# Expert rows in whole tiles of 256 and half tiles of 128, in place of whole tiles alone

## The chip, the core and the metric

The kernel runs on one NeuronCore of a Trainium2 chip. TensorE (PE) multiplies matrices and loads weights (PEld), VectorE (DVE), ScalarE (ACT) and GpSimd (POOL) work on elements, and SyncE (SP) issues most transfers. The metric is the device time of one execution, in microseconds (us). All data are fp32.

## The reference, cut to what matters

The reference is two layers of a model over 16 sequences of 569 rows (441 image tokens, 128 of text) with 256 columns: a tokenizer, windowed attention, a mixture of eight experts, a linear attention, and an LSTM over the 569 steps. The change is in the mixture of experts:

```python
xf = x.reshape(-1, Dd)                      # 9104 rows x 256
probs = jax.nn.softmax(xf @ gate_w + gate_b, axis=-1)
top2_vals, top2_idx = jax.lax.top_k(probs, 2)
cw = zeros.at[rows, top2_idx].add(top2_vals)
for w1, bb1, w2, bb2, we in zip(W1, b1, W2, b2, cw.T):   # 8 experts
    h = jax.nn.gelu(xf @ w1 + bb1)          # 256 -> 512
    y = h @ w2 + bb2                        # 512 -> 256
    acc = acc + we[:, None] * y
```

Only two of the eight weights `cw` of a row are not zero, so a kernel need run each row through two experts only.

## The kernel before

**Order of the work.** A first part (tokenizer, window attention, routing) holds about the first 950 us. It finds the two experts of every row and scatters each row, with its number, to the region of each expert in the DRAM tensor `XS` (L908, on POOL). Rows are padded to 72 chunks of 128, so there are 2 x 9216 = 18,432 rows for experts. Then the experts run, then the linear attention and the LSTM together to the end. The order of instructions on PE, DVE, ACT and POOL is written out when the program is built: a planner (`Order`) holds streams of steps with a cost each (`yield "PE", 0.43`) and picks the next step by the times at which engines come free. SP's order is the framework's. What runs is the order so built; engines wait on semaphores for what they need.

**Tiles.** How many rows an expert gets is known only at run time, but the number of tiles is fixed when the program is built. Each expert's rows are cut into tiles of `TILE` = 256. Eight experts can leave eight tiles partly filled, so `TILES` = 79 tiles are laid out, and all 79 always run.

**The plan of the tiles** (L1100 to L1155, on DVE) comes from `count`, the rows of each expert. `need` is the number of tiles of each expert and `end` its running sum. For every tile number, `past` marks the experts that end before it, so that its sum is the tile's `expert`, and `first` is its first row in `XS`. Both go to `where` as integers, which SP reads as register values (`planned`, L1158). The plan is worked out first for the four tiles that start, then for the other 75. `spare` gives row numbers to rows that hold nothing.

**A tile.** `tiles(slot)` is a stream; four of them (slots 0 to 3) take every fourth tile, and each has one PSUM bank. For a tile:

- SP loads `xs`, 256 rows of 258 columns (258 KB), and `w`, its expert's weights and biases (1154 KB), L1174 and L1168. Both have five buffers, so a tile's load waits for the tile five places earlier.
- PE turns the rows (`xtr`, four transposes, L1212), DVE copies them to `xt` (L1217). Four small DVE operations make the row numbers `to` (L1220 to L1233).
- The first layer, `hp` (L1241): the weights stand still and the 256 rows stream past, in two halves of four products each. After each half ACT applies gelu twice to give `hT` (L1248).
- The second layer, `y` (L1255): here 128 rows of `hT` stand still and the 256 columns of `w2` stream past, eight products.
- DVE adds the bias to give `ys` (L1261), and POOL scatters `ys` to the rows of `YT` in two indirect DMAs (L1184).

The linear attention's `front` later loads rows of `YT` (`yg`, L1353) and adds the two experts' results with their weights. `prepare` loads and prepares weights of later stages beside the experts.

Of the kernel before, what the change touches and what calls it, by code (L numbers as in the profile page):

```python
# [10 lines left out]
F32 = mybir.dt.float32  # L11
# [6 lines left out]
D = 256  # L18
# [3 lines left out]
E = 8  # L22
# [39 lines left out]

TILE = 256
REGION = [8 * 128 * len(g) + TILE for g in GROUPS]
TILES = [(2 * 8 * 128 * len(g) + E * (TILE - 1)) // TILE for g in GROUPS]
WPACK = 2 * HID + 4 + 4 * D + D

ROW = {n: i * D for i, n in enumerate(["bo", "b_out"])}
# [226 lines left out]
def kernel(ctx: ExitStack, tc: tile.TileContext, a: dict, out: bass.AP):  # L295
# [797 lines left out]
    def experts(g, mo, slots):  # L1093


        NT, most = TILES[g], E * REGION[g]
        bounded = "counts are bounded by the number of rows"

        behind = tiling.tile([128, E], mybir.dt.int32, name=f"behind{g}", tag="behind", bufs=1)
# [16 lines left out]
        warm = tiling.tile([128, 1], F32, name=f"warm{g}", tag="warm", bufs=1)  # L1116
        nc.scalar.activation(warm, count[:, :1], AF.Gelu)
        plan.table = "gelu"
        need = tiling.tile([128, E], F32, name=f"need{g}", tag="need", bufs=1)
        nc.vector.tensor_scalar(need, count, 1.0 / TILE, 0.5 - 0.5 / TILE, ALU.mult, ALU.add)  # L1120
        nc.vector.tensor_scalar(need, need, ROUND, None, ALU.add)
        nc.vector.tensor_scalar(need, need, ROUND, None, ALU.subtract)
        end = tiling.tile([128, E + 1], F32, name=f"end{g}", tag="end", bufs=1)
        nc.vector.memset(end[:, 0:1], 0.0)
        nc.vector.tensor_tensor_scan(end[:, 1:], ones[:, :E], need, 0.0, ALU.mult, ALU.add)
# [2 lines left out]
        first = tiling.tile([128, NT], F32, name=f"first{g}", tag="first", bufs=1)  # L1128
        where = tiling.tile([128, 2, NT], mybir.dt.int32, name=f"where{g}", tag="where", bufs=1)

        for lo, hi in ((0, slots), (slots, NT)):
            n, no = hi - lo, frow("tile_no", hi - lo, lo)
            past_, expert_, first_ = past[:, lo:hi], expert[:, lo:hi], first[:, lo:hi]
            nc.vector.tensor_tensor(
                past_, no.unsqueeze(2).to_broadcast([128, n, E]),
                end[:, 1:].unsqueeze(1).to_broadcast([128, n, E]), ALU.is_ge,
            )
            nc.vector.tensor_reduce(expert_, past_, AX.X, ALU.add)
            nc.vector.tensor_scalar(where[:, 1, lo:hi], expert_, float(E - 1), None, ALU.min)
            nc.vector.tensor_tensor(  # L1140
                past_, past_, need.unsqueeze(1).to_broadcast([128, n, E]), ALU.mult
            )
            nc.vector.tensor_reduce(first_, past_, AX.X, ALU.add)
            nc.vector.tensor_tensor(first_, no, first_, ALU.subtract)
            nc.vector.tensor_scalar(first_, first_, float(TILE), None, ALU.mult)
            nc.vector.scalar_tensor_tensor(
                first_, expert_, float(REGION[g]), first_, ALU.mult, ALU.add
            )
            nc.vector.tensor_scalar(where[:, 0, lo:hi], first_, float(most), None, ALU.min)

        spare = tiling.tile([128, 2, NT], F32, name=f"spare{g}", tag="spare", bufs=1)
        for i in range(2):
            nc.vector.tensor_scalar(
# [8 lines left out]

        loaded, bufs = [], slots + 1

        def weights(j, e=None):
            e = planned(1, j, j + 1, E - 1)[0] if e is None else e
            w = mo.tile([128, WPACK], F32, name=f"w{g}_{j}", tag="w", bufs=bufs)
            nc.sync.dma_start(w, a["wpack"][bass.ds(e, 1)].rearrange("e p n -> (e p) n"))  # L1168
            return w

        def load(j, w=None):
            at = planned(0, j, j + 1, most)[0]
            xs = mo.tile([128, 2, WIDE], F32, name=f"xs{g}_{j}", tag="xs", bufs=bufs)
            nc.sync.dma_start(xs, XS[g][bass.ds(at, TILE), :].rearrange("(i p) d -> p i d", p=128))  # L1174
            loaded.append((xs, weights(j) if w is None else w))

        ahead = [weights(j, e) for j, e in enumerate(planned(1, 0, 2, E - 1))]
# [1 line left out]
            load(j, ahead[j] if j < 2 else None)  # L1179

        def back_to_rows(j, ys, to):
            for i in range(2):
                yield "POOL", 1.27
                keep(nc.gpsimd.indirect_dma_start(  # L1184
                    out=YT, out_offset=bass.IndirectOffsetOnAxis(ap=to[:, i : i + 1], axis=0),
                    in_=ys[:, i, :], in_offset=None,
                ))
                nc.gpsimd.memset(between, 0.0)

        def tiles(slot):  # L1190
            for j in range(slot, NT, slots):
                while len(loaded) < min(j + 3, NT):
                    last = ("tile", g, len(loaded) - bufs)
                    if len(loaded) < bufs or last in plan.events:
                        load(len(loaded))
                    elif len(loaded) > j:
                        break
                    else:
                        yield "at", last
                yield "rank", j  # L1200
                xs, w = loaded[j]
                w1 = w[:, : 2 * HID].rearrange("p (k n) -> p k n", k=2)
                b1 = w[:, 2 * HID : 2 * HID + 4]
                w2 = w[:, 2 * HID + 4 : 2 * HID + 4 + 4 * D].rearrange("p (k n) -> p k n", k=4)
                b2 = w[:, 2 * HID + 4 + 4 * D :]
                if j < slots:
                    yield "pause", 5.0
                tr = bank(f"xtr{g}_{j}", slot).rearrange("p (k n) -> p k n", k=2)
                for k in range(2):
                    for i in range(2):  # L1210
                        yield "PE", TURN
                        nc.tensor.transpose(  # L1212
                            tr[:, k, 128 * i : 128 * i + 128], xs[:, i, 128 * k : 128 * k + 128], ident
                        )
                yield "DVE", 0.68
                xT = mo.tile([128, 2, TILE], F32, name=f"xt{g}_{j}", tag=f"xt{slot}", bufs=1)
                nc.vector.tensor_copy(xT, tr)  # L1217
                second = mo.tile([128, 2], F32, name=f"second{g}_{j}", tag=f"second{slot}", bufs=1)
                yield "DVE", 0.2
                nc.vector.tensor_scalar(  # L1220
                    second, xs[:, :, D + 1], expert[:, j : j + 1], float(KEPT),
                    ALU.not_equal, ALU.mult,
                )
                to = mo.tile([128, 2], mybir.dt.int32, name=f"to{g}_{j}", tag=f"rows{slot}", bufs=2)
                yield "DVE", 0.2
                nc.vector.tensor_tensor(second, second, xs[:, :, D], ALU.add)
                apart = mo.tile([128, 2], F32, name=f"apart{g}_{j}", tag=f"apart{slot}", bufs=1)
                yield "DVE", 0.2
                nc.vector.scalar_tensor_tensor(
                    apart, xs[:, :, D], 0.0, spare[:, :, j], ALU.is_equal, ALU.mult  # L1230
                )
                yield "DVE", 0.2
                nc.vector.tensor_tensor(to, second, apart, ALU.add)  # L1233
                hT = mo.tile([128, 4, TILE], F32, name=f"hT{g}_{j}", tag=f"hT{slot}", bufs=1)
                for half in range(2):
                    hp = bank(f"hp{g}_{j}_{half}", slot).rearrange("p (i n) -> p i n", i=2)
                    for i in range(2):
                        hc = 2 * half + i
                        for k in range(2):
                            yield "PE", 256 * COLUMN  # L1240
                            nc.tensor.matmul(  # L1241
                                hp[:, i, :], w1[:, k, hc * 128 : (hc + 1) * 128], xT[:, k, :],
                                start=(k == 0), stop=(k == 1),
                            )
                    for i in range(2):
                        hc = 2 * half + i
                        yield "ACT", 0.47, "gelu"
                        nc.scalar.activation(  # L1248
                            hT[:, hc, :], hp[:, i, :], AF.Gelu, bias=b1[:, hc : hc + 1]
                        )  # L1250
                y = bank(f"y{g}_{j}", slot).rearrange("p (i n) -> p i n", i=2)
                for i in range(2):
                    for hc in range(4):
                        yield "PE", 256 * COLUMN
                        nc.tensor.matmul(  # L1255
                            y[:, i, :], hT[:, hc, 128 * i : 128 * i + 128], w2[:, hc, :],
                            start=(hc == 0), stop=(hc == 3),
                        )
                yield "DVE", 0.69
                ys = mo.tile([128, 2, D], F32, name=f"ys{g}_{j}", tag=f"ys{slot}", bufs=2)  # L1260
                nc.vector.tensor_tensor(ys, y, b2.unsqueeze(1).to_broadcast([128, 2, D]), ALU.add)  # L1261
                plan.mark(("tile", g, j))
                plan.fork(back_to_rows(j, ys, to))

        return [tiles(slot) for slot in range(slots)]
# [810 lines left out]
```

## Time and profile before

| | |
|---|---|
| median of 3 runs | 3378.91 us (3378.6 to 3380.3) |
| profiled execution | 3360.87 us |
| its span, first to last instruction | 3359.0 us |
| mean TensorE clock granted | 0.978 |
| busy share of the span: PE, DVE, ACT, POOL | 91%, 60%, 44%, 23% |
| experts, first transpose to last `ys` | 972.8 to 1577 us |

A busy share is over the whole span; the stages differ. A row of the profile's groups gives the line, the engine, the operation with output and inputs, the count, the busy time and the mean of one instruction, and then the idle time just before, with what ended it. PE's records overlap, so that the time of a row of products is read from the step between their starts. An fp32 product of the code stands as two records, a transpose as one.

### The profile page before, as it was taken

Reading aid. Unit: us, or ns where it says so; the run is one execution under the profiler, and the core shown is the slowest. Engines: PE = TensorE matmul, PEld = TensorE weight load, DVE = VectorE, ACT = ScalarE, POOL = GpSimd, SP = SyncE. Lnnn points to the kernel's source line nnn. Section 1 sums busy time; section 2 is a strip of 40 time slices with the busy share of each in tenths; the row PEclk is TensorE's granted clock in tenths of the full one; section 3 lists DMA queues with packets and bytes.
Section 4 is the critical chain, followed back from the end, with each engine's and each line's share of the span. In section 5 each row is a group of like instructions: output and inputs, shape, how many; then the busy total and the mean of one; then the engine's idle time right before and its main releaser. Section 6 shows DMA issues by size and latency. Waiting matters only on the chain.

```text
span 3359.0 us, 134328 instructions
## 1 busy us (share of the span) xinstructions
PE 3055.1 (91%) x57536; PEld 2231.5 (66%) x57536; DVE 2027.2 (60%) x6787; ACT 1471.9 (44%) x5030; POOL 786.6 (23%) x1524
## 2 busy tenths in 40 slices
PE   5999999999859999997899999999999999999884
PEld 3666666666548888886566676766666666666652
DVE  4677777766732222222566777777777777766555
ACT  3545545454412222221444555555555555554442
POOL 1243554445533322232311001010101010100000
PEclk9999999999979999998999999999999999999997
DMA  5111221111176666664333333333333333333333
GB/s 180 53 46 57 89 79 54 55 38 41 42 251 234 220 231 225 225 229 141 100 100 88 90 82 86 84 94 78 97 77 92 84 93 79 76 91 80 90 103 113
DMA packets 276070, 366.81 MB, mean 109 GB/s; under 512 B 144480, under 2 KB 220176, under 8 KB 263312
## 3 DMA queue, kind: packets, MB, share of 16 engines
q1 hardware_dynamic: 249360, 300.91, 30.5%
q0 software_dynamic: 14496, 39.75, 3.1%
q10 hardware_dynamic: 11616, 17.56, 1.8%
q8 instruction: 451, 7.39, 0.9%
q14 instruction: 147, 1.20, 0.1%
HBM read 239.33 MB, written 118.75 MB: 107 GB/s over the span
## 4 chain that ended last, share of the span: by engine, by line
PE 37%; DVE 7%; ACT 5%; issue 2%; SPq 1%; DMA 1%; POOL 0%; ACTq 0%; DVEq 0%; POOLq 0%
PE gates L1741 13%; PE xm_False L1085 5%; PE out_gate L1750 2%; PE ek L1085 2%; PE po_False L1085 2%; PE z L1085 2%; PE v L1085 2%; PE eq L1085 2%; PE ds_False L1085 2%; ACT act L1762 1%; PE r_False L1085 1%; ACT th L1798 1%; DVE ab L1777 1%; DVE cT L1790 1%; DVE act L1783 1%
## 5 line engine op out<-in xcount | busy, mean ns | idle before, releaser
L1741 PE MATMUL gates<-W_hh,X 128*16 128x96 f32 (+1 forms) x18176 | 487.9, 248 | 63.9 <-DVE X L1805 61.6
L1741 PEld LDWEIGHTS gates<-W_hh,X 128*16 128x16 f32 (+1 forms) x18176 | 373.6, 103 | 258.5 <-DVE X L1805 245.0
L1248 ACT ACTIVATE hT<-hp,w 128x256 f32<-128x256 f32 x316 | 132.6, 472 | 481.5 <-PE hp L1241 314.5
L1762 ACT ACTIVATE act<-gates 128x96 f32<-128x96 f32 x568 | 142.1, 250 | 444.1 <-PE gates L1741 437.0
L1255 PE MATMUL y<-w,hT 128*128 128x256 f32 x1264 | 289.7, 382 | 5.2 <-ACT hT L1248 1.5
L1085 PE MATMUL xm_False<-W_ih,dxT_False 128*32 128x256 f32 x4352 | 292.3, 380 | 2.3 <-DVE dxT_False L1271 1.9
L1241 PE MATMUL hp<-xt,w 128*128 128x256 f32 x1264 | 287.6, 381 | 1.0 <-ACT hT L1248 1.0
L1777 DVE SCALAR_TENSOR_TENSOR ab<-act 128x64 f32<-128x64 f32 x568 | 127.9, 225 | 258.2 <-ACT act L1762 250.8
L1255 PEld LDWEIGHTS y<-w,hT 128*128 128x128 f32 x1264 | 236.8, 190 | 45.2 <-ACT hT L1248 14.4
L1684 PEld LDWEIGHTS <-nil 128*32 128x32 bf16 x4552 | 190.3, 94 | 111.0 <-issue 53.0
L1241 PEld LDWEIGHTS hp<-xt,w 128*128 128x128 f32 x1264 | 239.9, 191 | 35.7 <-ACT hT L1248 1.5
L1184 POOL DMA_INDIRECT YT<-ys,to x158 | 153.4, 971 | 440.4 <-DVE ys L1261 408.9
L1261 DVE TENSOR_TENSOR ys<-y,w 128x512 f32<-128x512 f32 x79 | 54.6, 691 | 316.3 <-PE y L1255 241.1
L1750 PE MATMUL out_gate<-W_hh,X 128*32 128x64 f32 x9088 | 233.8, 219 | 0.7 <-issue 0.7
L1690 ACT COPY gates<-xc 128x96 f32<-128x96 f32 x569 | 138.6, 244 | 182.0 <-DMA xc<-XCD 75.4
L1750 PEld LDWEIGHTS out_gate<-W_hh,X 128*32 128x32 f32 x9088 | 187.9, 110 | 2.9 <-issue 1.1
L1805 DVE SCALAR_TENSOR_TENSOR X<-toT,th 128x32 f32<-128x32 f32 x569 | 109.9, 193 | 120.5 <-ACT th L1798 116.9
L1798 ACT ACTIVATE th<-cT 128x32 f32<-128x32 f32 x569 | 130.5, 229 | 92.9 <-DVE cT L1790 43.1
L1301 POOL TENSOR_SCALAR d_False_rstd<-d_False_mv 128x2 f32<-128x2 f32 (+1 forms) x36 | 9.0, 250 | 671.8 <-DVE d_False_mv L1293 547.4
L908 POOL DMA_INDIRECT XS<-XN,at x144 | 149.1, 1035 | 45.6 <-issue 24.6
L693 PE MATMUL wqk<-wxT,wqkv 128*128 128x128 f32 x1152 | 150.6, 278 | 8.9 <-ACT wxT L687 8.6
L693 PEld LDWEIGHTS wqk<-wxT,wqkv 128*128 128x128 f32 x1152 | 139.4, 192 | 24.9 <-ACT wxT L687 13.5
(356 smaller groups left out, 6497.9 us busy)
## 6 DMA issues: line engine op xcount, KB each, us to landing
w<-in_wpack SPq DMA_DIRECT2D x79, 1154.0 KB
taps<-in_taps SPq DMA_DIRECT2D x16, 1764.0 KB
xc<-XCD SPq DMA_DIRECT2D x71, 384.0 KB
XCD<-xp_False SPq DMA_DIRECT2D x256, 96.0 KB
xs<-XS SPq DMA_DIRECT2D x79, 258.0 KB
yg<-YT SPq DMA_DIRECT2D x72, 256.0 KB
HD<-h SPq DMA_DIRECT2D x72, 128.0 KB
fh<-HD SPq DMA_DIRECT2D x72, 128.0 KB
```

The costliest lines, as they stand in the source:

```text
L693: nc.tensor.matmul(qk[:, j, m, :], wqkv[:, k, D * j + 128 * m : D * j + 128 * m + 128], xT[:, k, :], start=(k == 0), stop=(k == 1),)
L908: fill(0, nc.gpsimd.indirect_dma_start(out=XS[0], out_offset=bass.IndirectOffsetOnAxis(ap=at[:, i, c - lo : c - lo + 1], axis=0), in_=XN[p ...
L1085: nc.tensor.matmul(out[own], lhsT[:, own], rhs, start=start, stop=stop)
L1184: keep(nc.gpsimd.indirect_dma_start(out=YT, out_offset=bass.IndirectOffsetOnAxis(ap=to[:, i : i + 1], axis=0), in_=ys[:, i, :], in_offset= ...
L1241: nc.tensor.matmul(hp[:, i, :], w1[:, k, hc * 128 : (hc + 1) * 128], xT[:, k, :], start=(k == 0), stop=(k == 1),)
L1255: nc.tensor.matmul(y[:, i, :], hT[:, hc, 128 * i : 128 * i + 128], w2[:, hc, :], start=(hc == 0), stop=(hc == 3),)
L1684: nc.tensor.matmul(g[32 * q : 32 * q + 32, :n], nil[:, :32], nil[:, :n], start=True, stop=last)
L1741: nc.tensor.matmul(GC[32 * q : 32 * q + NB * (1 + half), :96], before[:, kk, NB * (1 - half) :], Whh[:, kk, own : own + 96], start=False, ...
L1750: nc.tensor.matmul(GO[32 * q : 32 * q + 32, :64], before[:, kk, :], Whh[:, kk, own : own + 64], start=False, stop=(kk == 1),)
L1762: nc.scalar.activation(act[:, :96], GC[:, :96], AF.Tanh, scale=0.5), begun.pop((k, t))
L1777: nc.vector.scalar_tensor_tensor(ab, act[:, :64].rearrange("p (g x) -> p g x", g=2), 1.0, act[:, 64:].rearrange("p (g x) -> p g x", g=2), ...
L1798: nc.scalar.activation(th.rearrange("p k x -> p (k x)"), cT, AF.Tanh, scale=0.5)
```

## The change

Experts' rows are cut into half tiles of 128 rows. Of each expert as many whole tiles of 256 as fit (`need`, now half of `halves` rounded down) come first. At least 68 whole tiles exist whatever the counts, so 68 whole tiles and 15 half tiles are laid out (`WHOLE` = 68, `TILES` = 83) and all 83 run. The half tiles take what the 68 whole ones leave: `left` is the number of halves of each expert that no whole tile holds. Their plan is a third block on DVE, after the blocks of 4 and of 64 whole tiles.

The 15 half tiles (numbers 68 to 82) are spread by `order`: the first comes after tile 7, then one after every four whole tiles, the last before tile 64. The loads, the slots and the planner's ranks go by the place in this order, no more by the number of the tile. A half tile loads 128 rows and its expert's full weights, and does two transposes, `hp` with 128 columns, four `y` products and one scatter. The planner's costs are scaled to match.

```diff
-TILES = [(2 * 8 * 128 * len(g) + E * (TILE - 1)) // TILE for g in GROUPS]
+WHOLE = [(2 * 8 * 128 * len(g) - E * TILE // 2 + TILE - 1) // TILE for g in GROUPS]
+TILES = [
+    w + (2 * 8 * 128 * len(g) + E * (TILE // 2 - 1)) // (TILE // 2) - 2 * w for w, g in zip(WHOLE, GROUPS)
+]
...
+        half = TILE // 2
+        halves = tiling.tile([128, E], F32, name=f"halves{g}", tag="halves", bufs=1)
         need = tiling.tile([128, E], F32, name=f"need{g}", tag="need", bufs=1)
-        nc.vector.tensor_scalar(need, count, 1.0 / TILE, 0.5 - 0.5 / TILE, ALU.mult, ALU.add)
-        nc.vector.tensor_scalar(need, need, ROUND, None, ALU.add)
-        nc.vector.tensor_scalar(need, need, ROUND, None, ALU.subtract)
+        for to, x, by, off in (
+            (halves, count, 1.0 / half, 0.5 - 0.5 / half), (need, halves, 0.5, -0.25)
+        ):
+            nc.vector.tensor_scalar(to, x, by, off, ALU.mult, ALU.add)
+            nc.vector.tensor_scalar(to, to, ROUND, None, ALU.add)
+            nc.vector.tensor_scalar(to, to, ROUND, None, ALU.subtract)
...
-        for lo, hi in ((0, slots), (slots, NT)):
+        for lo, hi in ((0, slots), (slots, whole)):
...
+        n, no = NT - whole, frow("tile_no", NT - whole)
+        past_, expert_, first_ = past[:, whole:], expert[:, whole:], first[:, whole:]
...
+        nc.vector.tensor_scalar(begin, end, float(whole), 2.0, ALU.min, ALU.mult)
+        nc.vector.memset(used[:, E:], 0.0)
+        nc.vector.tensor_tensor(used[:, :E], begin[:, 1:], begin[:, :E], ALU.subtract)
+        nc.vector.tensor_tensor(left, halves, used[:, :E], ALU.subtract)
+        nc.vector.tensor_tensor_scan(end[:, 1:], ones[:, :E], left, 0.0, ALU.mult, ALU.add)
...
+        nc.vector.tensor_scalar(where[:, 0, whole:], first_, float(most), None, ALU.min)
...
+        def rows_in(j):
+            return 2 if j < whole else 1
+
+        each = (whole - 2 * slots) / (NT - whole)
+        order = sorted(
+            range(NT), key=lambda j: j if j < whole else 2 * slots - 0.5 + (j - whole) * each
+        )
...
-        def load(j, w=None):
+        def load(n, w=None):
+            j = order[n]
...
-            nc.sync.dma_start(xs, XS[g][bass.ds(at, TILE), :].rearrange("(i p) d -> p i d", p=128))
+            n = rows_in(j)
+            nc.sync.dma_start(
+                xs[:, :n, :], XS[g][bass.ds(at, 128 * n), :].rearrange("(i p) d -> p i d", p=128)
+            )
...
-            for i in range(2):
+            for i in range(rows_in(j)):
                 yield "POOL", 1.27
...
-            for j in range(slot, NT, slots):
-                while len(loaded) < min(j + 3, NT):
+            for at, j in list(enumerate(order))[slot::slots]:
+                while len(loaded) < min(at + 3, NT):
...
                 for k in range(2):
-                    for i in range(2):
+                    for i in range(n):
                         yield "PE", TURN
...
-                            yield "PE", 256 * COLUMN
+                            yield "PE", 128 * n * COLUMN
                             nc.tensor.matmul(
-                                hp[:, i, :], w1[:, k, hc * 128 : (hc + 1) * 128], xT[:, k, :],
+                                hp[:, i, : 128 * n], w1[:, k, hc * 128 : (hc + 1) * 128], xT[:, k, :],
                                 start=(k == 0), stop=(k == 1),
...
-                        yield "ACT", 0.47, "gelu"
+                        yield "ACT", 0.25 + 0.11 * n, "gelu"
...
-                for i in range(2):
+                for i in range(n):
                     for hc in range(4):
                         yield "PE", 256 * COLUMN
...
-                yield "DVE", 0.69
+                yield "DVE", 0.14 + 0.275 * n
...
-                plan.mark(("tile", g, j))
+                plan.mark(("tile", g, at))
```

More of the change, by code (lines that the diff above doesn't have):

```diff
@@ L1093, in experts @@
     def experts(g, mo, slots):
-        NT, most = TILES[g], E * REGION[g]
+        NT, whole, most = TILES[g], WHOLE[g], E * REGION[g]
         bounded = "counts are bounded by the number of rows"
@@ L1149, in experts @@
             nc.vector.tensor_scalar(where[:, 0, lo:hi], first_, float(most), None, ALU.min)
+        n, no = NT - whole, frow("tile_no", NT - whole)
+        past_, expert_, first_ = past[:, whole:], expert[:, whole:], first[:, whole:]
+        used = tiling.tile([128, E + 1], F32, name=f"used{g}", tag="used", bufs=1)
+        begin = tiling.tile([128, E + 1], F32, name=f"begin{g}", tag="begin", bufs=1)
+        left = tiling.tile([128, E], F32, name=f"left{g}", tag="left", bufs=1)
+        nc.vector.tensor_scalar(begin, end, float(whole), 2.0, ALU.min, ALU.mult)
[3 more added lines that the diff above has]
+        nc.vector.tensor_tensor_scan(end[:, 1:], ones[:, :E], left, 0.0, ALU.mult, ALU.add)
+        nc.vector.tensor_tensor(begin[:, 1:], used[:, 1:], used[:, :E], ALU.subtract)
+        nc.vector.tensor_tensor(begin[:, 1:], begin[:, 1:], left, ALU.subtract)
+        nc.vector.tensor_tensor(
+            past_, no.unsqueeze(2).to_broadcast([128, n, E]),
+            end[:, 1:].unsqueeze(1).to_broadcast([128, n, E]), ALU.is_ge,
+        )
+        nc.vector.tensor_reduce(expert_, past_, AX.X, ALU.add)
+        nc.vector.tensor_scalar(where[:, 1, whole:], expert_, float(E - 1), None, ALU.min)
+        nc.vector.tensor_tensor(
+            past_, past_, begin[:, 1:].unsqueeze(1).to_broadcast([128, n, E]), ALU.mult
+        )
+        nc.vector.tensor_reduce(first_, past_, AX.X, ALU.add)
+        nc.vector.tensor_tensor(first_, no, first_, ALU.add)
+        nc.vector.tensor_scalar(first_, first_, used[:, :1], float(half), ALU.add, ALU.mult)
+        nc.vector.scalar_tensor_tensor(
+            first_, expert_, float(REGION[g]), first_, ALU.mult, ALU.add
+        )
+        nc.vector.tensor_scalar(where[:, 0, whole:], first_, float(most), None, ALU.min)
         spare = tiling.tile([128, 2, NT], F32, name=f"spare{g}", tag="spare", bufs=1)
@@ L1163, in experts @@
         loaded, bufs = [], slots + 1
+        def rows_in(j):
[3 more added lines that the diff above has]
+            range(NT), key=lambda j: j if j < whole else 2 * slots - 0.5 + (j - whole) * each
+        )
         def weights(j, e=None):
@@ L1169, in weights @@
             return w
-        def load(j, w=None):
+        def load(n, w=None):
+            j = order[n]
             at = planned(0, j, j + 1, most)[0]
             xs = mo.tile([128, 2, WIDE], F32, name=f"xs{g}_{j}", tag="xs", bufs=bufs)
-            nc.sync.dma_start(xs, XS[g][bass.ds(at, TILE), :].rearrange("(i p) d -> p i d", p=128))
+            n = rows_in(j)
+            nc.sync.dma_start(
+                xs[:, :n, :], XS[g][bass.ds(at, 128 * n), :].rearrange("(i p) d -> p i d", p=128)
+            )
             loaded.append((xs, weights(j) if w is None else w))
@@ L1195, in tiles @@
                         load(len(loaded))
-                    elif len(loaded) > j:
+                    elif len(loaded) > at:
                         break
@@ L1199, in tiles @@
                         yield "at", last
-                yield "rank", j
-                xs, w = loaded[j]
+                yield "rank", at
+                xs, w = loaded[at]
+                n = rows_in(j)
                 w1 = w[:, : 2 * HID].rearrange("p (k n) -> p k n", k=2)
@@ L1214, in tiles @@
                         )
-                yield "DVE", 0.68
+                yield "DVE", 0.14 + 0.27 * n
                 xT = mo.tile([128, 2, TILE], F32, name=f"xt{g}_{j}", tag=f"xt{slot}", bufs=1)
-                nc.vector.tensor_copy(xT, tr)
+                xT = xT[:, :, : 128 * n]
+                nc.vector.tensor_copy(xT, tr[:, :, : 128 * n])
                 second = mo.tile([128, 2], F32, name=f"second{g}_{j}", tag=f"second{slot}", bufs=1)
@@ L1220, in tiles @@
                 nc.vector.tensor_scalar(
-                    second, xs[:, :, D + 1], expert[:, j : j + 1], float(KEPT),
+                    second[:, :n], xs[:, :n, D + 1], expert[:, j : j + 1], float(KEPT),
                     ALU.not_equal, ALU.mult,
@@ L1225, in tiles @@
                 yield "DVE", 0.2
-                nc.vector.tensor_tensor(second, second, xs[:, :, D], ALU.add)
+                nc.vector.tensor_tensor(second[:, :n], second[:, :n], xs[:, :n, D], ALU.add)
                 apart = mo.tile([128, 2], F32, name=f"apart{g}_{j}", tag=f"apart{slot}", bufs=1)
@@ L1229, in tiles @@
                 nc.vector.scalar_tensor_tensor(
-                    apart, xs[:, :, D], 0.0, spare[:, :, j], ALU.is_equal, ALU.mult
+                    apart[:, :n], xs[:, :n, D], 0.0, spare[:, :n, j], ALU.is_equal, ALU.mult
                 )
                 yield "DVE", 0.2
-                nc.vector.tensor_tensor(to, second, apart, ALU.add)
+                nc.vector.tensor_tensor(to[:, :n], second[:, :n], apart[:, :n], ALU.add)
                 hT = mo.tile([128, 4, TILE], F32, name=f"hT{g}_{j}", tag=f"hT{slot}", bufs=1)
@@ L1246, in tiles @@
                         hc = 2 * half + i
-                        yield "ACT", 0.47, "gelu"
+                        yield "ACT", 0.25 + 0.11 * n, "gelu"
                         nc.scalar.activation(
-                            hT[:, hc, :], hp[:, i, :], AF.Gelu, bias=b1[:, hc : hc + 1]
+                            hT[:, hc, : 128 * n], hp[:, i, : 128 * n], AF.Gelu, bias=b1[:, hc : hc + 1]
                         )
                 y = bank(f"y{g}_{j}", slot).rearrange("p (i n) -> p i n", i=2)
-                for i in range(2):
+                for i in range(n):
                     for hc in range(4):
@@ L1258, in tiles @@
                         )
-                yield "DVE", 0.69
+                yield "DVE", 0.14 + 0.275 * n
                 ys = mo.tile([128, 2, D], F32, name=f"ys{g}_{j}", tag=f"ys{slot}", bufs=2)
-                nc.vector.tensor_tensor(ys, y, b2.unsqueeze(1).to_broadcast([128, 2, D]), ALU.add)
-                plan.mark(("tile", g, j))
+                nc.vector.tensor_tensor(
+                    ys[:, :n], y[:, :n], b2.unsqueeze(1).to_broadcast([128, n, D]), ALU.add
+                )
+                plan.mark(("tile", g, at))
                 plan.fork(back_to_rows(j, ys, to))
```

## The prediction

> **What bounds the kernel now.** I read the page's groups first, to find the lines that the change touches, then the busy time by stretches, then the instructions of one loop turn in order of time, and last who waits for whom.
>
> The groups (line, engine, operation, tiles, count | busy, mean ns | idle before):
>
> ```profile
> L1255 PE MATMUL y<-w,hT 128*128 128x256 f32 x1264 | 289.7, 382 | 5.2 <-ACT hT L1248 1.5
> L1241 PE MATMUL hp<-xt,w 128*128 128x256 f32 x1264 | 287.6, 381 | 1.0 <-ACT hT L1248 1.0
> L693 PE MATMUL wqk<-wxT,wqkv 128*128 128x128 f32 x1152 | 150.6, 278 | 8.9 <-ACT wxT L687 8.6
> L693 PEld LDWEIGHTS wqk<-wxT,wqkv 128*128 128x128 f32 x1152 | 139.4, 192 | 24.9 <-ACT wxT L687 13.5
> ```
>
> The two expert products have 1264 records each, 16 per tile of 79: every fp32 product that the code writes is two records. L693 belongs to another stage; it shows the same product at 128 columns instead of 256, each with its own weights, which is what a half tile's first layer will be. Busy time of PE, PEld, DVE, ACT, POOL, clock, DMA share and GB/s, by stretches:
>
> ```profile
> 972.00:1000.00 28.00, 25.65 (x113) 22.14 (x114) 6.43 (x24) 5.75 (x14) 4.29 (x8) 0.84 0.80 283
> 1000.00:1540.00 540.00, 535.07 (x2576) 464.44 (x2575) 131.37 (x453) 119.26 (x284) 166.47 (x304) 1.00 0.67 228
> 1540.00:1577.00 37.00, 33.77 (x158) 28.37 (x156) 6.75 (x20) 7.56 (x18) 9.99 (x20) 1.00 0.20 67
> ```
>
> The experts run from 972.8 to 1577, 18% of the span. In their middle PE is busy 535 of 540 us, the transfers 0.67. One loop turn, PE alone (start, duration):
>
> ```profile
> 1194.85 0.81 PE L1241 MATMUL hp<-xt,w 128*128 128x256 f32 x3
> 1195.50 1.04 PE L1212 MATMUL xtr<-ident,xs 128*128 128x128 f32 x8
> 1196.64 3.72 PE L1255 MATMUL y<-w,hT 128*128 128x256 f32 x16
> 1200.20 3.19 PE L1241 MATMUL hp<-xt,w 128*128 128x256 f32 x14
> 1203.22 3.62 PE L1255 MATMUL y<-w,hT 128*128 128x256 f32 x16
> 1206.68 4.05 PE L1241 MATMUL hp<-xt,w 128*128 128x256 f32 x18
> ```
>
> The transposes at 1180.44 and at 1195.50 are one turn apart: 15.06 us for two tiles, **7.53 us a tile**. Records overlap; what counts is the step between starts. 18 products in 4.05 with the last one 0.38 long: 3.67 / 17 = 0.2155 us a record. 8 transposes: (1.04 - 0.27) / 7 = 0.109. A tile is then 32 x 0.2155 + 4 x 0.109 = 7.33 us of PE, and 0.20 is left over. 0.27 per turn of that stands before the y at 1196.64, where PE waits for ACT's gelu; the rest is 0.065 a tile. So in this stage PE's rows are the time, and the next stage starts when the last YT rows have landed.
>
> Who waited, in SP's own waits from 1000 to 1560 (total, times, longest), and, ahead of the stage, from 940 to 975:
>
> ```profile
> SPq L1168 <- DVE ys L1261: 402.1, 71, 6.9
> ```
>
> ```profile
> SPq L1158 <- DVE where L1149: 11.8, 1, 11.8
> SPq L1168 <- DMA XS<-XN,at: 10.1, 5, 3.3
> ```
>
> SP waits for a buffer to come free before nearly every weight load: loads are ahead of PE, not behind it.
>
> **What the Trainium skill says.** "TensorE: Matmul & The Clock Gate", Back-to-back issue gap, gives a warm step of N / 2.4 + 2.5 ns, nearly proportional to the columns N. The trace agrees in form at two passes per record: 256 columns would be 216 ns (measured 215.5), 128 would be 109. Its part What happens when you issue a matmul, first step, says that the next weights load while the present matmul runs; here the 192 ns loads of L693 run under steps shorter than they are (below). "DMA: Bandwidth & Descriptors", Anatomy of one DMA, puts about 2 us on a transfer beside its bytes, measured for GpSimd's path; the loads here are SP's, and for them I use what this trace shows, 5.1 us in all for an xs (below).
>
> **The change, part by part.** 68 whole and 15 half tiles are 19,328 rows, 79 whole ones 20,224: 11 whole tiles go, 15 half tiles come.
>
> *A half tile on PE.* First layer: 8 products, 16 records of 128 columns. Their step is measured on L693, 16 records in one run:
>
> ```profile
> 442.48 2.00 PE L693 MATMUL wqk<-wxT,wqkv 128*128 128x128 f32 x16
> ```
>
> (2.00 - 0.275) / 15 = 0.115; an 18-record run (2.17) and a 1.95 one give 0.1115, which I take. 16 x 0.1115 = 1.78. Second layer: the weights and rows change places, so it stays at 256 columns and halves in number: 8 x 0.2155 = 1.72. Transposes 2 x 0.109 = 0.22. Sum **3.73 us**, against 7.33.
>
> *A turn.* In the changed kernel's instruction order a turn is four whole tiles and one half: 4 x 7.33 + 3.73 = 33.05. Waits for gelu: in the turn shown above the y at 1196.64 came 1.57 us after PE had issued the last hp it needs (1191.62, the start of the 18-run before it, + 16 x 0.2155 = 1195.07), with 1.30 of other work between (two records and 8 transposes), because a gelu of the next tile sits between its own two on ACT. In the new turn one y has this pattern and only two records and 6 transposes between, 1.08: it waits 0.49. The other four have 1.29 or more between and need two gelus running, 1.57 - 0.42 = 1.15: no wait. Leftover 5 x 0.065 = 0.3. Turn: 33.05 + 0.5 + 0.3 = 33.85. 15 turns 507.8, the other 8 whole tiles 8 x 7.53 = 60.2, together 568.0. Before: 79 x 7.53 = 594.9. **Gain 26.9 us.**
>
> *The plan of the tiles on DVE.* Three more 128x8 operations ahead of the first `where` (0.16 to 0.17 each): 0.5 us later. Then a block of 64 instead of 75 columns (0.1 less on each of four) and 16 small operations for the half tiles, about 3.2 us. Hidden: the first weight load waits until 963.4 for the XS rows to land, while the first `where` was there at 952.5, so some 10 us cover the 0.5; DVE's next work is xt at 973.9, the plan ends about 960. Without that cover the 0.5 would count. Taken as 0, bounds 0 to +0.5. POOL's scatter to XS waits for the cast of `at`, which stands one place earlier in DVE's order: 0.
>
> *SP and the transfers.* Four more tiles are 8 more DMAs with as many register loads; SP stands idle 402 us, so 0. One Wq load moves ahead of the first w, into SP's wait from 940.7: 0. Bytes per tile 1.18 MB of weights whole or half, 0.264 or 0.132 of rows in and about as much out. Weights +4.7 MB, rows -1.8: about 2% more bytes in 568 instead of 595 us, the share goes from 0.67 to 0.72. The shortest lead is that of the third whole tile of a group of three: its xs is issued after the ys of the tile six places earlier. From that y's end PE does hp 1.72, 0.89, 0.43, y 3.45, hp 0.89, 1.29, y 1.72, hp 1.72 and 8 transposes 0.87, 13.0 us; less ys (0.9 with its hop) and SP's load of w before it (0.8) leaves 11.3 us. An xs needed 5.1 us in the flood at the start (xs of tile 3 issued 972.00, PE's transposes of it at 977.09, four weight loads about it, share 0.80). So 6 us in hand: 0, and for the worst see the rivals.
>
> *ACT, DVE and POOL inside the stage.* Half-size gelu, copies and adds, 151 scatters for 158: these engines are busy 22, 24 and 31%, all less than before. 0.
>
> *After the experts.* The last four tiles are whole as before, so the tail (last y, ys, two scatters, the yg loads) is the same. PE's, ACT's and POOL's order in the LSTM stage is unchanged; on DVE six operations of one front, and one yg load on SP, come a few places later, once. They stand beside a chain of gates with waits of 100 us and more on those streams: 0, bounds -1 and +2.
>
> Sum: -26.9. The profiled run took 3360.87 (span 3359.0 + 1.9), 18 us less than the median 3378.91 of the three runs (3378.6 to 3380.3). I take the difference over to the median: **3352.0**.
>
> **The rivals.**
> 1. *Gelu waits vanish altogether* in the new order (leftovers too): 15 x 33.05 + 8 x 7.33 = 554.4, which is 40 less; half of that extra is as far as I believe: 3345. For it: longer runs of transposes. Against it: order on ACT. Chance 0.12.
> 2. *A 128-column step limited by its weight load*, 0.190 instead of 0.1115, if the w tile's loads don't overlap as L693's do: 15 x 16 x 0.0785 = 18.8 back, gain 8: 3371. Against it: L693 has the same 192 ns loads with other weights each time. Chance 0.07, with half steps between.
> 3. *The loads become the bound, and the kernel slower.* A half tile's weights come for half the PE time: its bytes, 1.45 MB at 339 GB/s (228 at a share of 0.67), are 4.3 us of transfer for 3.73 of PE. If the third xs of each group landed later than its lead, PE would stop once a turn. It eats the gain at 26.9 / 15 = 1.8 us a turn, that is a landing 13.1 us after issue, and is slower by 0.2% from 13.6 us; at 14.5 it gives 15 x 3.2 = 48, so 3400. For it: five weight loads in 33.85 us instead of 4.5. Against it: over a turn 24.5 us of transfer in 33.85, and the 5.1 us at the start. Chance 0.05.
> 4. *The half tiles do less than said*: if the planner had put them together rather than spread, waits for weights would follow; the built order shows one per turn, so this falls under 3.
>
> Likeliest, as computed, with losses of a few us from transfers or the later stage: 0.76, 3346 to 3360.
>
> **How the numbers follow.** A run of this kernel can tell about 0.2%, 6.8 us. Low end 3343: rival 1 and a little. High end 3365: N = 128 at 0.125 (+3.2), half a us of xs wait a turn (+8), +2 from the LSTM stage. Faster by over 0.2% (below 3372.1): all but rival 3 and the tail of 2: 0.93; same 0.03; slower 0.04.
>
> **What would show it.** Page after: 1328 hp records (68 x 16 at 256 columns, 15 x 16 at 128) and 1208 y records (68 x 16 + 15 x 8), the 128-column ones stepping 0.11; five tiles in 33.9 us; the stage from 973 to about 1550; PE's wait for xs only at the start; SP still waiting for ys. Wrong if PE waits for xs or w in each turn, if the first xtr comes later than 973.5, or if the LSTM stage's length changes by over 3 us.

## The result, and the profile after

| | before | after |
|---|---|---|
| median of 5 runs | 3378.91 us | 3349.33 us |
| lowest to highest | 3378.2 to 3382.1 | 3346.3 to 3353.5 |
| ratio, 95% interval | | 0.9913 [0.9899, 0.9927] |
| profiled execution (span) | 3360.87 (3359.0) | 3353.51 (3351.6) |

The change takes 29.6 us off; 26.9 were forecast. The two profiled executions differ by only 7 us: that of before was 18 us under its median and that of after the slowest of its five. So their spans are not subtracted here; they are read stage by stage.

The page's groups of after, the two expert products (count | busy, mean ns | idle before):

```profile
L1306 PE MATMUL y<-w,hT 128*128 128x256 f32 x1208 | 276.3, 381 | 6.9 <-ACT hT L1299 6.4
L1292 PE MATMUL hp<-xt,w 128*128 128x256 f32 (+1 forms) x1328 | 275.2, 360 | 0.0
```

1208 and 1328 records are the numbers forecast. The second form of `hp` is the 128-column one. The page now names gelu for 6.4 us of waits at L1306, where it named it for 1.5 at L1255. That is not more waiting in all: the 0.27 that a turn of before loses at one `y` leaves gaps too short for the page to name. By the prediction's readings 39 such turns lose about 10.5 us (an estimate), and 15 turns of after at 0.49 lose about 7.4.

The middle of the stage by the busy-time view (PE, PEld, DVE, ACT, POOL, clock, DMA share, GB/s):

```profile
1000.00:1540.00 540.00, 535.05 (x2717) 471.87 (x2716) 139.11 (x497) 126.75 (x318) 167.47 (x305) 1.00 0.70 243
```

PE is as full as before (535.05 against 535.07 us of 540), and the transfers' share went from 0.67 to 0.70.

PE alone in order of time, one turn of four whole tiles and one half (start, duration, and in brackets the idle time before):

```profile
1225.42 2.35 PE L1292 MATMUL hp<-xt,w 128*128 128x128 f32 x14
...
1245.76 2.32 PE L1292 MATMUL hp<-xt,w 128*128 128x256 f32 x10
1247.92 0.82 PE L1262 MATMUL xtr<-ident,xs 128*128 128x128 f32 x6
1249.06 3.72 PE L1306 MATMUL y<-w,hT 128*128 128x256 f32 x16 [0.32 <-ACT hT L1299]
1252.61 3.21 PE L1292 MATMUL hp<-xt,w 128*128 128x256 f32 x18
1255.67 3.62 PE L1306 MATMUL y<-w,hT 128*128 128x256 f32 x16
1259.12 2.35 PE L1292 MATMUL hp<-xt,w 128*128 128x128 f32 x14
```

The row of `hp` with the half tile's columns comes again after 1259.12 - 1225.42 = **33.70 us**. Inside it one `y` waits: it starts 1.14 after the six transposes before it, which take 6 x 0.109 = 0.65, so 0.49 is lost (the view counts 0.32 of it).

Who waits in the stage: PE over the whole of it, then SP from 1010 to 1540 (total, times, longest):

```profile
PE xtr L1262 <- DMA xs<-XS: 25.9, 2, 24.3
PE y L1306 <- ACT hT L1299: 6.4, 16, 1.0
```

```profile
SPq L1213 <- DVE ys L1312: 370.7, 76, 8.2
```

PE waits for rows twice, both at the start of the stage. SP still waits for a free buffer before nearly every weight load.

### The profile page after: what moved, and what is told of

It reads as the page before. It is cut to its first block, busy times and chain, and to the rows that moved or that the text cites. A ratio compares the mean times of both kernels' runs of the same rounds, so it can differ in the third digit from the quotient of the medians.

```text
span 3351.6 us, 134422 instructions
## 1 busy us (share of the span) xinstructions
PE 3040.4 (91%) x57530; PEld 2219.1 (66%) x57530; DVE 2032.9 (61%) x6830; ACT 1471.1 (44%) x5046; POOL 779.9 (23%) x1510
## 4 chain that ended last, share of the span: by engine, by line
PE 37%; DVE 7%; ACT 5%; issue 2%; SPq 1%; DMA 1%; POOL 0%; ACTq 0%; DVEq 0%
PE gates L1794 13%; PE xm_False L1088 5%; PE out_gate L1803 2%; PE ek L1088 2%; PE z L1088 2%; PE v L1088 2%; PE ds_False L1088 2%; PE eq L1088 1%; PE po_False L1088 1%; ACT act L1815 1%; PE r_False L1088 1%; ACT th L1851 1%; DVE ab L1830 1%; DVE cT L1843 1%; DVE act L1836 1%
## 5 line engine op out<-in xcount | busy, mean ns | idle before, releaser
L1299 ACT ACTIVATE hT<-hp,w 128x256 f32<-128x256 f32 (+1 forms) x332 | 132.6, 452 | 449.2 <-PE hp L1292 337.0
L1306 PE MATMUL y<-w,hT 128*128 128x256 f32 x1208 | 276.3, 381 | 6.9 <-ACT hT L1299 6.4
L1292 PE MATMUL hp<-xt,w 128*128 128x256 f32 (+1 forms) x1328 | 275.2, 360 | 0.0
L1312 DVE TENSOR_TENSOR ys<-y,w 128x512 f32<-128x512 f32 (+1 forms) x83 | 53.4, 643 | 358.7 <-PE y L1306 325.7
L1306 PEld LDWEIGHTS y<-w,hT 128*128 128x128 f32 x1208 | 226.3, 190 | 41.6 <-ACT hT L1299 11.2
L1292 PEld LDWEIGHTS hp<-xt,w 128*128 128x128 f32 x1328 | 232.8, 190 | 28.7 <-ACT hT L1299 0.2
```

The costliest lines, as they stand in the source:

```text
L1292: nc.tensor.matmul(hp[:, i, : 128 * n], w1[:, k, hc * 128 : (hc + 1) * 128], xT[:, k, :], start=(k == 0), stop=(k == 1),)
L1306: nc.tensor.matmul(y[:, i, :], hT[:, hc, 128 * i : 128 * i + 128], w2[:, hc, :], start=(hc == 0), stop=(hc == 3),)
```

## The experiments

Times are compared within one group of runs, which share their runs of before; the medians of before in the groups lie up to 15 us apart. The time of before_again, after_again, four_more_whole and of the last three is that of a single execution, the others are medians. Stages are compared between all, each from the one profiled execution: "experts" is from the start of the first transpose to the start of the last `ys`.

| kernel | time | before beside it | experts | last cast of `at` to first weight load, and on to first transpose | first `ftr` to end |
|---|---|---|---|---|---|
| before, profiled first | 3378.91 | | 603.6 | 12.7 + 9.4 | 1766 |
| after, profiled first | 3349.33 | 3378.91 | 570.7 | 12.5 + 10.0 | 1773 |
| before_again | 3380.02 | 3383.51 | 604.4 | 12.9 + 9.4 | 1771 |
| after_again | 3350.59 | 3383.51 | 573.0 | 14.6 + 10.1 | 1773 |
| wide_first_layer | 3390.24 | 3383.51 | 607.9 | 14.0 + 10.1 | 1768 |
| halves_last | 3354.03 | 3383.51 | 578.8 | 13.9 + 10.3 | 1780 |
| after_clock0 | 3338.19 | 3368.76 | 570.7 | 13.4 + 10.2 | 1776 |
| after_paired | 3339.24 | 3368.76 | 573.9 | 13.6 + 10.1 | 1776 |
| more_halves | 3401.10 | 3368.76 | 629.5 | 13.1 + 10.1 | 1779 |
| four_more_whole | 3402.87 | 3368.76 | 633.2 | 13.0 + 9.4 | 1776 |
| longer_plan | 3368.21 | 3370.15 | 603.2 | 12.7 + 10.0 | 1773 |
| late_half_plan | 3340.42 | 3370.15 | 572.2 | 13.2 + 9.3 | 1776 |
| before_third | 3364.21 | 3370.15 | 603.6 | 12.8 + 9.4 | 1769 |

**Each kernel once more** (before_again, after_again, unaltered).

> The kernel before, unchanged, profiled once more to see how much each stage varies between executions. If the stages repeat, the experts again take 603.6 us from the first transpose of rows to the last bias add, and whatever the time differs by lies in the first part (972.8 us in the first profile) or after the experts (1782.6). If the experts' own length moves by several us, the split of the gain by stages cannot be trusted.

> The changed kernel, unchanged, profiled once more. The first profile had the experts at 570.7 us, the first part at 991.8 and the rest at 1789.1, 19.0 and 6.5 longer than before. If these two are chance, the experts repeat within 1 us and the other two stages come closer to those of the kernel before. If they belong to the change (a later order of DVE, tensors placed elsewhere), they repeat.

The experts take 604.4 and 573.0: over three executions of each, after_paired and before_third below included, the stage repeats within 1 us for before and within 3 for after. The spread lies in its first 28 us. PE's first long row of products and the third tile's first `y`, in the first profiles of before and of after:

```profile
978.00 8.23 PE L1241 MATMUL hp<-xt,w 128*128 128x256 f32 x30
999.68 3.72 PE L1255 MATMUL y<-w,hT 128*128 128x256 f32 x16
```

```profile
996.64 6.67 PE L1292 MATMUL hp<-xt,w 128*128 128x256 f32 x30
1016.75 3.72 PE L1306 MATMUL y<-w,hT 128*128 128x256 f32 x16
```

The same 30 records take 8.23 us in one and 6.67 in the other. The third tile's first `y` comes 26.9, 27.9 and 26.8 us after the first transpose in the three executions of before, and 25.0, 27.3 and 28.0 in those of after. The clock granted over the first 14 us of the stage was 0.70, 0.63 and 0.71, and 0.88, 0.67 and 0.63: the higher it was, the earlier that `y` came. From that `y` to the last `ys` the stage takes 576.7, 576.5 and 576.8 us in before and 545.7, 545.8 and 546.0 in after. **30.9 us** is what the change takes off there, and it repeats to 0.3.

The part ahead of the experts, in which the two kernels run nearly the same order of work, repeats less: the first transpose came at 972.8 and 987.1 us in these two executions of before, at 991.8 and 985.8 in the two of after. Kernels of one group lie closer: 985.8 to 989.4 in the group of before_again, 975.2 to 980.6 in that of after_paired, 973.5 to 974.6 in that of before_third, with both plans in each. So nothing shows that the late start in the first profile of after belongs to the change.

**Half tiles with a full first layer** (wide_first_layer): a half tile turns its 128 rows twice and sends all 256 columns through `hp` and gelu; only `y` and the scatter stay halved.

```diff
-                    for i in range(n):
+                    for i in range(2):
...
-                            yield "PE", 128 * n * COLUMN
+                            yield "PE", 256 * COLUMN
...
-                                hp[:, i, : 128 * n], w1[...], xT[:, k, :],
+                                hp[:, i, :], w1[...], xT[:, k, :],
```

> Half tiles whose first layer streams 256 columns after all: the 128 rows are transposed twice, gelu runs at full size, the second layer stays at 4 products. If PE's rows are the time of this stage, each half tile costs 16 x (0.2155 - 0.1115) + 2 x 0.109 = 1.88 us more, 28 us in all: experts about 599, time about 3377, the gain gone. If the weight loads set the step of these products, or the transfers set the stage, the columns cost little: time within 5 us of the changed kernel's 3349.

Experts 607.9, 36 more than the mean of after and after_again, where 28 were expected. Two steps of PE alone:

```profile
1231.88 1.04 PE L1262 MATMUL xtr<-ident,xs 128*128 128x128 f32 x8
...
1245.21 1.04 PE L1262 MATMUL xtr<-ident,xs 128*128 128x128 f32 x8
...
1260.27 1.04 PE L1262 MATMUL xtr<-ident,xs 128*128 128x128 f32 x8
```

Two whole tiles take 1260.27 - 1245.21 = 15.06, as in before. A whole one with a half takes 1245.21 - 1231.88 = 13.33, so this half takes 13.33 - 7.53 = 5.80; in after it adds 33.70 - 4 x 7.53 = 3.58. The 2.22 between them are 16 records at 256 instead of 128 columns, 16 x (0.2155 - 0.1115) = 1.66, two more transposes, 0.22, and the gelu waits that this order has in each pair of tiles; 15 x 2.22 = 33 of the 36. Bytes and weight loads per half tile are the same as in after, so it is not the loads that the half tile saves but what streams, with the transposes and gelu that go with it: at 256 columns again the whole gain is gone (1.0019 [1.0009, 1.0029] of before). A 128-column step held at 0.190 by its weight load would have left 16 x 0.0255 = 0.41 of the 1.66.

**All half tiles at the end** (halves_last): `order = list(range(NT))`.

> The same 68 whole and 15 half tiles with the half tiles all after the whole ones. PE's rows are the same. If spreading them is only a precaution, the experts stay within 3 us of 570.7. If loads fall behind where half tiles stand together (4.3 us of transfer for 3.7 of PE each, five buffers ahead), the stage grows by about 15 x 0.6 = 8 us, and PE waits for xs or w in it; if each half tile then waits for the whole landing of its load, by 25 us or more, time 3375.

Experts 578.8, 7 more than after. PE alone near the end, and the busy-time view of the middle and of the end:

```profile
1512.88 2.17 PE L1290 MATMUL hp<-xt,w 128*128 128x128 f32 x18
...
1538.25 0.46 PE L1290 MATMUL hp<-xt,w 128*128 128x128 f32 x2 [0.38 <-DMA w<-in_wpack]
...
1551.45 0.41 PE L1260 MATMUL xtr<-ident,xs 128*128 128x128 f32 x2 [1.43 <-DMA xs<-XS]
```

```profile
1000.00:1500.00 500.00, 495.03 (x2383) 429.59 (x2383) 121.02 (x418) 112.19 (x268) 154.65 (x283) 1.00 0.67 226
1500.00:1560.00 60.00, 57.59 (x381) 53.13 (x380) 16.89 (x80) 17.59 (x56) 17.33 (x32) 1.00 0.83 303
```

Here 18 half-tile records stand in one row: (2.17 - 0.275) / 17 = **0.1115 us** a record, which is the step that the prediction took from L693 (the form in the Trainium skill's "TensorE: Matmul & The Clock Gate", Back-to-back issue gap, gives 109 ns for two passes, as an estimate; the section calls this form that of an isolated product and puts about 81 ns at 128 columns on a stream of weight loads and products, which would be an estimated 162 for two passes. Here the measured 0.1115 decides, and it lies near the first). Side by side the half tiles ask for 303 GB/s, share 0.83, and PE waits once for a `w` and once for an `xs`. So the mechanism of rival 3 exists, but mildly, and with half tiles next to each other: the waits for loads that the view names in this stretch are 0.38 and 1.43, under 2 of the 7 us. The growth comes near the 8 us expected, but mostly not for the reason given there; the rest is not placed. In the whole time the 7 us are within the spread: 0.9905 [0.9888, 0.9922].

**The order after the experts** (after_clock0, with after_paired beside it). The change also moved six vector operations and one `yg` load in the LSTM stage. One line shifts the planner's clock when the experts end, and the LSTM stage gets the order of before again on every engine:

```diff
         tiling.release()
+        plan.free = {e: t - max(plan.free.values()) + 600.0 for e, t in plan.free.items()}
```

> The changed kernel's experts stage, with the kernel before's order of instructions in the LSTM stage on every engine (one added line shifts the planner's clock at the end of the experts, so that a near tie falls as it did before). Theory A, the six vector operations and the one yg load that came a few places later cost something: ftr to the end goes from the 1773 us of the changed kernel back to the 1766 to 1771 of the old order, and the kernel is 2 to 5 us faster than the changed one timed beside it, about 3345. Theory B, the reorder is free as predicted: experts 572 us, the LSTM stage anything between 1766 and 1774 as in executions of one program, time equal to the changed kernel within 2 us.

> The changed kernel unaltered, beside the others. Both theories: 3350 us within 3, 0.991 of the time before, experts 571 to 573 us. It is the yardstick for the order of the LSTM stage: A has it 2 to 5 us above its twin with the old order there, B within 2.

From the first `ftr` to the end both take 1776 us, and the medians are 3338.19 (0.9911 [0.9895, 0.9928]) and 3339.24 (0.991 [0.9894, 0.9927]). This pair shows no cost of the reorder. It does not exclude the 2 to 5 us of theory A, as each interval is 11 us wide. And the other executions lean the other way: with the order of before on DVE, ACT, POOL and SP this part took 1766 to 1776 us (before three times, wide_first_layer, longer_plan, after_clock0; mean 1770.5), with the order of after 1773 to 1776 (after three times, late_half_plan; mean 1774.6). As after_clock0 took 1776 with the old order, the order alone does not explain this, and the cause stays open. Over all thirteen executions the part takes 1766 to 1780 us, and 1766, 1771 and 1769 for before alone.

**The price of a half tile and of a whole one** (more_halves: 14 more half tiles, 29 in 97; four_more_whole: the kernel before with 83 whole tiles). The added tiles hold no row.

> The changed kernel with 14 more half tiles, 29 in all, spread in the same way; the added ones hold no row. The price of a half tile by itself. Columns alone: 14 x 3.73 us = 52 us, experts 572 + 52 = 624. The net price read from the changed kernel's turn (33.70 less four whole tiles at 7.53): 14 x 3.58 = 50, experts 622. If the loads bind, a wait for xs or w beside each half tile, with two half tiles for every four whole ones or so the share goes from 0.70 to about 0.76: experts above 635 and waits for xs or w in the middle of the stage. About 3400 us in the first cases.

> The kernel before with 83 whole tiles in place of 79 (the four more hold no row). Price of a whole tile by itself: 4 x 7.53 = 30 us, experts 604 + 30 = 634. Against the 572 of 83 tiles of which 15 are half this gives what halving a tile saves: (634 - 572) / 15 = 4.1 us, where the prediction's 7.53 - 3.73 and the gelu wait of 0.5 gave 3.5 (33.85 a turn against 5 x 7.53 = 37.65: 3.8). If a tile's cost is not PE's rows but its loads, the four cost less than 25.

Four whole tiles cost 633.2 - 603.9 (mean of three executions of before) = 29.3. From the third tile's first `y` on, where the stage repeats better, they cost 606.5 - 576.7 = 29.8, 7.45 each: a whole tile has its price of 7.5 by itself, and the four don't come under the 25 us that were expected if the loads set it. Laid against the mean experts stage of after, 572.5 (570.7, 573.0, 573.9), halving 15 of 83 tiles saves (633.2 - 572.5) / 15 = 4.05 each, where the prediction's sums gave 3.8 for a tile in its turn; the measured turn gives (5 x 7.53 - 33.70) = 3.95.

In more_halves a half tile follows every two whole ones. PE alone, three places:

```profile
1107.72 1.09 PE L1262 MATMUL xtr<-ident,xs 128*128 128x128 f32 x4 [5.08 <-DMA xs<-XS]
...
1228.54 1.26 PE L1262 MATMUL xtr<-ident,xs 128*128 128x128 f32 x10
...
1247.11 1.25 PE L1262 MATMUL xtr<-ident,xs 128*128 128x128 f32 x10
```

The steady turn is 1247.11 - 1228.54 = 18.57 for two whole tiles and a half, with no gelu wait. The prediction's sum gives 2 x 7.33 + 3.73 = 18.39 of PE work, so 0.06 a tile is left over. The stage took 629.5 where 622 to 624 were expected, and 5.08 of that is one wait, at 1107.72. Without it, and from the third tile's first `y` on, the 14 half tiles cost (603.0 - 545.8 - 5.1) / 14 = 3.72 each, the 3.73 of the columns. The wait does not look like one for bandwidth. DVE's and then SP's instructions ahead of it (start, duration, in brackets the idle time before):

```profile
1090.54 0.27 DVE L1060 MEMSET l_bo<- 128x256 uint32 x1
1096.35 0.28 DVE L1065 CAST l_bo_pieces<-flow 1x256 bf16<-1x256 f32 x1 [5.54 <-DMA l_bv<-l_bv_pieces]
...
1097.77 0.67 DVE L1312 TENSOR_TENSOR ys<-y,w 128x512 f32<-128x512 f32 x1
```

```profile
1089.35 3.76 SPq L1071 DMA_DIRECT2D l_bv<-l_bv_pieces  x6
1093.63 0.36 SPq L1221 DMA_DIRECT2D xs<-XS  x1
1096.66 3.68 SPq L1071 DMA_DIRECT2D l_bo<-l_bo_pieces  x6
1101.29 0.35 SPq L1213 DMA_DIRECT2D w<-in_wpack  x1
```

The vector engine waits 5.54 for six transfers of 0.5 KB by `prepare` to land. Behind that cast in its order stands the `ys` of a `y` that PE had finished at 1091.14 (its row of 16 starts at 1087.52 and lasts 3.62). So `ys` comes 6.6 late, its buffer is free as much later, and SP, which has six more small transfers to issue first, loads the next `w` at 1101.29. In after DVE waits 5.57 at the same cast, and PE's next rows are there in time. In before DVE waits 7.58 there, and PE 1.34 behind it:

```profile
1103.74 0.28 DVE L1062 CAST l_bo_pieces<-flow 1x256 bf16<-1x256 f32 x1 [7.58 <-DMA l_bv<-l_bv_pieces]
1105.89 0.66 PE L1212 MATMUL xtr<-ident,xs 128*128 128x128 f32 x4 [1.34 <-DVE ys L1261]
```

No run moves these transfers, so this chain is read from the traces and not tested. The transfers' share in the steady stretch is 0.73, less than the 0.83 of halves_last, where the waits were shorter.

**Between the routing and the first transpose** (longer_plan: before, with three idle vector operations ahead of the first tile numbers and sixteen after the plan; late_half_plan: after, with the half tiles' block of the plan moved behind the row numbers of the fifth tile; before_third: before).

```diff
+        def plan_halves():
+            n, no = NT - whole, frow("tile_no", NT - whole)
...
+                if at == 4:
+                    yield "DVE", 3.2
+                    plan_halves()
```

> The kernel before with the added work on the vector engine alone: three idle 128x8 operations before the first tile numbers and sixteen of the sizes of the half tiles' plan after them, results unused, 79 whole tiles. It asks where some 1.4 us between the last cast of the routing and the first transpose come from: 22.1 to 22.4 us in three executions with the plan of before, 22.5 to 24.7 (mean 23.7) in seven with the plan of after; 9.4 against 10.1 of it lies between the first weight load and the first transpose. Theory A, the longer plan slows the last scatter to XS and what follows: 23.2 to 24.2, the last scatter 1.15 us instead of 0.96. Theory B, the longer plan is hidden as predicted and the difference is in the loads (their order or their addresses): 22.1 to 22.5, with 9.4 in its second part. Experts 604, about 3375 either way.

> The changed kernel with the half tiles' block of the plan moved behind the row numbers of the fifth tile, so that it is out of the way while the rows are scattered. Theory A: the last cast to the first transpose goes from 23.7 back to about 22.4, last scatter 0.96 us. Theory B: 23 to 24.5 as before the move, with 10.1 of it after the first weight load. Experts 570 to 574 either way, as DVE is busy a quarter of that stage; about 3345.

> The kernel before once more, beside the other two: last cast to first transpose 22.1 to 22.4, 9.4 of it after the first weight load, experts 604. Both theories say the same of it; it is their yardstick.

The second part, first weight load to first transpose, behaves as theory A says: 10.0 with idle operations added to before, 9.3 with the block moved out of the way in after, 9.4 in before. The first part does not: 12.7, 13.2 and 12.8. Together longer_plan's 22.7 lies between what the two theories gave it. Nor is it the last scatter, as A had it: that took 1.43 in longer_plan, 1.16 in late_half_plan and 0.96 in before_third. The DMA view between the first weight load and the first transpose (queue, kind: packets, MB, share), first longer_plan, then before_third:

```profile
q1 hardware_dynamic: 1126, 3.41, 90.6%
q14 instruction: 1, 0.01, 0.2%
q10 hardware_dynamic: 5, 0.00, 0.1%
```

```profile
q1 hardware_dynamic: 1072, 3.17, 90.1%
```

The row of q10 does not go with the time: late_half_plan has nine of its packets, at 9.3. That of q14 does. One packet of instructions is fetched in that stretch in the eight executions where it takes 10.0 us or more (after and its variants but late_half_plan, and longer_plan), and in none of the five where it takes 9.3 or 9.4. That the added instructions bring the fetch into the stretch is shown. That the fetch is what costs the 0.7 us, and how, is not: it came and went together with the added vector operations.

## Why the prediction was right

- **A half tile's price** (3.73: 1.78 + 1.72 + 0.22). Right. The 0.1115 of L693 is the half tile's own step to the digit, and in more_halves the added half tiles cost 3.72 each.
- **A turn** (33.05 + 0.5 + 0.3 = 33.85). Measured 33.70. The one gelu wait is there, once a turn, at 0.49; the leftover is 0.15, not 0.3, so the 0.065 a tile of before is not a constant of every tile. Over 15 turns: 2.25 us more gain. (3.67 / 17 is 0.2159, not the 0.2155 that the prediction wrote; that is 0.01 us a tile.)
- **568.0 against 594.9.** The turns give 15 x 33.70 + 8 x 7.53 = 565.7, a gain of 29.2. The stage itself gained 603.9 - 572.5 = 31.4; 0.4 of that is the difference in the first 28 us (27.2 against 26.7 in the mean), and 30.9 came off behind them. Some 1.6 of the other 1.7 are waits that a count by turns leaves out: in before the last tile's transposes stand alone, with 0.54 for gelu after them, and one transpose early in the stage waits 1.2 to 1.6 for a `ys`; in after the 0.54 is gone and the wait for `ys` is at most 0.6.
- **The plan on DVE** (0, bounds 0 to +0.5). This term was mis-sized. The 10 us of cover were there for the `where` values, but with the longer plan 0.6 to 0.7 us more pass elsewhere, between the first weight load and the first transpose. The stretch before that load took 12.7 to 13.0 in four executions of the plan of before and 12.5 to 14.6 in seven of after; whether the change has a part in it stays open.
- **SP and the transfers** (0, share 0.72). Right: 0.70, and no wait for rows or weights after the start. That the lead of 11.3 us and the landing of 5.1 are what they were put at is not measured. What the prediction had not named is that a `ys`, and with it a free buffer, can be held up by another stream's wait on DVE; as the traces read, this cost 1.3 us once in before and 5 in more_halves.
- **After the experts** (0, bounds -1 and +2). Not settled. Giving the old order back changed nothing that the runs can tell, yet the part took 1769 us in the mean of three executions of before and 1774 in that of three of after. "Wrong if the LSTM stage changes by over 3 us" could not tell, since one program varies by 5. Nor could "first transpose later than 973.5": one program varies by 14.
- **Rivals.** 1 (gelu waits vanish): one remains per turn. 2 (weight loads hold the step at 0.190): refuted by the 0.1115 in place. 3 (loads bind): not in after; seen mildly in halves_last. 4: the tiles are halved as said.
- **The total.** The medians gave -29.6, -29.5 (after_paired) and -30.6 (after_clock0), each with an interval of about 5 us to either side. The profiled executions give -31.4 in the experts, about +1.4 between the routing and them and, unexplained, +5 behind them, together -25, which lies at the edge of the first interval (24.7 to 34.1 us off). The experts' share is known to about a microsecond. That the forecast of the whole came within 3 us is in part luck: the terms that it put at 0 move by more than that from one execution to another.

No kernel here beats after by more than the runs can tell: after_clock0 has the same time.

## What to carry to other kernels

When a stage is full of matmul rows, price a padding change by columns: count records, take the step of a same-shaped row anywhere in the trace, add the one wait that the new order shows. This is shown here for 256 and 128 columns and no further down: L876 in before, with 72 columns and weights as large, has its second record 0.105 after its first, where 72 / 128 of 0.1115 would be 0.063 (an estimate); why is not shown. Halving a tile halves only what streams; its weights still come whole, so put half tiles among whole ones, where the transfers' share was 0.70, rather than side by side, where it was 0.83 and PE waited twice for loads. Before reading a small difference between two profiles, see how far that stage differs between two executions of one program, and compare from a point on from which they agree.

## What was not expected of the hardware

- Nearly the same instructions ahead of the experts took 972.8 to 987.1 us in three executions of before and 980.6 to 991.8 in three of after; the experts repeat to 0.3 us once their first 28 us are left out, and those go with the clock granted over the first 14, which was 0.63 to 0.88.
- One fetched packet of instructions between the first weight load and the first transpose goes with 0.6 us and more there, in eight executions of eight; that it is the cause is not shown.
- Weight loads of 0.190 us in the trace do not hold back a row of matmuls that steps every 0.1115.
